# A fused dilated attention and depthwise convolution: the convolution's centre term moved into PSUM, one block's left column moved to VectorE, the exponentials kept in PSUM, and a new order of all stages

## The chip, the cores and the metric

The kernel runs on one core of a Trainium2 chip. The core has five engines with a queue each: TensorE (PE in the profile; its weight loads are PEld), VectorE (DVE), ScalarE (ACT), GpSimd (POOL) and SyncE (SP), which here issues nearly all DMAs. The metric is the device time of one execution in microseconds. Before the change it is 5062.4 us, the median of three runs (5062.21 to 5062.62). A profile is one further execution, recorded by the hardware profiler.

## The reference

Two layers on an image batch `x` of 16 x 56 x 56 x 384 in float32:

```python
    # --- layer 0 (conv_preact) ---
    x = x + _L0_conv_ref(_gn(x), L0_conv_w_qkv, L0_conv_w_proj, L0_conv_b_proj)
    # --- layer 1 (conv_preact) ---
    x = x + _L1_conv_ref(_gn(x), L1_conv_w)
```

`_gn` is a group norm over 32 groups of channels. Layer 0 is a dilated neighbourhood attention: q, k and v are products of the normalised `x` with `w_qkv`; the 384 channels are three groups of 128 (four heads of 32 channels each) with dilations 1, 2 and 3; each pixel attends to the 3 x 3 neighbours at its group's distance,

```python
        attn = jnp.einsum('bgdn,bgdkn->bgnk', qg, ku) * scale
        attn = jax.nn.softmax(attn, axis=-1)
        out = jnp.einsum('bgnk,bgdkn->bgnd', attn, vu)
```

and the result goes through `w_proj` and `b_proj`. Layer 1 is a 3 x 3 depthwise convolution (one kernel per channel) whose weights are the signs of `w`.

## The kernel before

Channels lie on the 128 partitions, in three blocks (j = 0, 1, 2). A chunk is 8 rows of 56 pixels, 448 in all; an image has 7 chunks, the batch 112. A chunk goes through three plans. Plan A (`plan_a`) loads it and turns it to channels first (pt_x, xa) and sends it to DRAM as xd, with running statistics. Plan B (`plan_b`) is the attention; plan C (`plan_c`), some ten chunks later, the convolution.

Plan B, for each of three channel groups: `k_or_v` and `query` are products of three matmuls each on TensorE (L526), into a PSUM tile pkv (pool `ps_mt`) or pq (pool `ps_q`). `score` multiplies pq with three neighbours of k at once on VectorE (t, L591: 1344 elements a partition). `score_rounds` sums each head's 32 channels of t by narrow matmuls into ps (L572; 128x32, four beside each other in the array). `softmax` copies ps (L611), turns it (pt_s, L615), takes the maximum and the difference on VectorE (L620, L621), the exponential on ScalarE (L623), the sum, its reciprocal and the product on VectorE (L627, L628, L630); then the weights are split into three bf16 terms (L633, L636, L640, L641) and turned by a DMA into aT (L644). `weigh`, once for each row of neighbours (i = 0 to 8), spreads the weights over the channels on TensorE into pb_a (L658; pool `ps_bc`, three banks, a single buffer), multiplies by v on VectorE (w, L669) and adds up on GpSimd (L679, L682, L683). `out_project` multiplies with w_proj (po, L696), adds bias and residual (L701), takes statistics (L705) and sends x1 to DRAM.

Plan C: `load` brings each 32 channels of block 0 and 1 three times, shifted by a row (z), `normalise` normalises z on ScalarE (L786). `convolve` makes the left and right columns of the 3 x 3 kernel for blocks 0 and 1 on TensorE: for each of the two columns kx = 0 and 2, and each quarter q, one matmul (pc, L817; 96 rows by 32 columns of the array). The middle column (upper and lower tap: L828, L831) is added on VectorE, on raw x1 with scalars cs that hold kernel times group-norm scale. `column` computes the centre tap with the group norm's offset and the residual on ScalarE into an SBUF tile u (L807), and VectorE adds it last (L834). Block 2 is done without TensorE: nine scaled copies on ScalarE (L881) that GpSimd adds (L891, L896, L899). `turn` turns the result back (pt_o, L908) and writes it out.

[...]The eight banks are: `ps_mt` three (pkv, pt_x, pt_s, po, pc, pt_o and small products of the group norm), `ps_q` one, `ps_s` one (ps, and later the sums psm), `ps_bc` three. A tile that takes a bank waits until the one that had it was read.

The order is written out. `WHEN` gives each stage a place in units of which nine make a chunk (`STEP`); `put` adds these to a chunk's start t0 and splits a stage at its `yield`s. All pieces are sorted by place; between places `FROM` and `UNTIL` every engine's instructions are chained in that order (`pin`), SP's DMAs included. Before the change that is so from chunk 0 on, FROM = 0; pieces with places under 0 or past UNTIL are left to the scheduler. The last image's convolution has its places by itself, after the last statistics, and lies past UNTIL.

Of the kernel before, what the change touches and what calls it, by code (L numbers as in the profile page):

```python
# [8 lines left out]
F32 = mybir.dt.float32  # L9
BF16 = mybir.dt.bfloat16  # L10
I32 = mybir.dt.int32
AF = mybir.ActivationFunctionType
ALU = mybir.AluOpType
# [9 lines left out]
NQ = 4  # L23
ROWS = 8
# [10 lines left out]
    load_in=[[16.753]],  # L35
    turn_in=[[17.144, 17.155, 17.527, 18.442], [18.901, 18.912, 18.923, 27.065], [19.007, 19.044, 19.055,
        19.119]],
    load_x=[[-8.992]],
    normalise=[[-7.557], [-6.631], [-8.034]],
    k=[[-1.772, -1.287, -0.448], [0.602, 0.693, 0.86], [1.389, 1.4, 3.364]],  # L40
    v=[[8.754, 8.765, 10.709], [11.496, 11.507, 13.768], [11.843, 12.429, 17.643]],
    query=[[8.972], [10.387], [12.844]],
    score=[[9.067], [9.078], [9.773], [10.398], [11.394], [12.106], [13.128], [13.334], [13.447]],
    burst=[[10.996], [12.316], [15.131]],
    softmax=[[15.921, 17.148, 17.159, 17.17, 18.062, 18.073, 18.4, 18.411, 18.491, 18.969]],
    weigh=[[20.479, 20.601, 20.612], [20.873, 21.461, 23.801], [21.808, 22.007, 26.039], [23.6, 23.611, 26.895],
        [24.179, 25.026, 27.192], [25.361, 26.931, 28.274], [26.999, 27.767, 29.055], [28.005, 28.036, 29.926],
        [28.762, 28.913, 30.376]],
    load_residual=[[33.194]],
    out_project=[[30.892, 34.249, 34.26, 121.395], [30.995, 34.02, 34.806, 62.468], [36.328, 36.339, 36.805,  # L50
        37.381]],
    load_g=[[15.738]],
    normalise_g=[[20.315]],
    taps=[[23.621, 25.792], [23.781, 25.945], [23.792, 25.956]],
    sums=[[26.625], [26.636], [26.647]],
    load_x1=[[12.088]],
    load_z=[[4.532, 8.639], [18.154, 18.373]],
    normalise_z=[[11.361, 11.372], [19.211, 19.222]],
    column=[[12.191], [16.571]],
    convolve=[[12.055, 12.746], [20.473, 20.484]],  # L60
    turn_out=[[27.033, 27.07, 27.117], [27.209, 27.576, 27.587], [27.767, 27.778, 29.092], [28.344, 28.355,
        36.059]],
    statistics=[[38.5, 42.48, 42.607, 43.359, 44.23, 44.622, 44.633, 44.887, 45.025, 45.117, 45.558, 45.569,
        45.58, 46.991, 47.002]],
# [6 lines left out]
def dilated_attention_then_binary_conv(  # L71
# [48 lines left out]
    ps_mt = ctx.enter_context(tc.tile_pool(name="ps_mt", bufs=3, space=PSUM))  # L120
    ps_q = ctx.enter_context(tc.tile_pool(name="ps_q", bufs=1, space=PSUM))
# [54 lines left out]
    kcol = const.tile([P, JG, 3], F32, name="kcol")  # L176
# [18 lines left out]
    u_p = ctx.enter_context(tc.tile_pool(name="u_p", bufs=1))  # L195
# [79 lines left out]
    def small_weights():  # L275
# [34 lines left out]
        nc.vector.tensor_add(kcol[:, :, 2], up, mid)  # L310
        eye3 = raw["eye"]
# [15 lines left out]
    def rows(ap):  # L327
        return ap.rearrange("p (r w) -> p r w", w=W)
# [114 lines left out]
    def must_hold(what, value):  # L443
        assert holds.get(what) == value, (what, holds.get(what), value)
# [63 lines left out]
    def plan_b(m, t0):  # L508
# [88 lines left out]
        def by_neighbour(ap):  # L597
            return ap.rearrange("p s (o k) -> p s o k", o=NTAP)

        def over_neighbours(ap):  # L600
            return ap.unsqueeze(2).to_broadcast([SUB, NSUB, NTAP, GH])
# [5 lines left out]
        def softmax():  # L607
# [9 lines left out]
            must_hold("ew", m - 1 if m else None)  # L617
# [3 lines left out]
            nc.vector.tensor_tensor(by_neighbour(weights), by_neighbour(pt4), over_neighbours(mx), ALU.subtract)  # L621
            yield
            nc.scalar.activation(weights, weights, AF.Exp, scale=SCALE)  # L623
            yield
            sm = ps_s.tile([P, 512], F32, tag="s", name="psm")[:SUB, : NSUB * GH]
            sm = sm.rearrange("p (s k) -> p s k", s=NSUB)
            nc.vector.reduce_sum(sm, by_neighbour(weights).rearrange("p s o k -> p s k o"), axis=AX.X)  # L627
            nc.vector.reciprocal(sm, sm)  # L628
            yield
            nc.vector.tensor_tensor(by_neighbour(weights), by_neighbour(weights), over_neighbours(sm), ALU.mult)  # L630
# [91 lines left out]
    def column_scalars(b):  # L722

        mr = mr1[b][0]
        cs = st_p.tile([P, JG, 6], F32, tag="cs", name="cs")
        nc.gpsimd.tensor_tensor(
            cs[:, :, 0:3], ktap[:, :JG, 1:NTAP:3], mr[:, :JG, 1:2].to_broadcast([P, JG, 3]), ALU.mult
        )
        nc.gpsimd.tensor_tensor(cs[:, :, 3:6], kcol, mr[:, :JG, 0:1].to_broadcast([P, JG, 3]), ALU.mult)
        nc.gpsimd.tensor_scalar(cs[:, :, 1], cs[:, :, 1], 1.0, None, op0=ALU.add)  # L730
        cs1[b] = cs

    def plan_c(m, t0):
# [17 lines left out]
        def set_of(j, q):  # L751
            return next(z[:, q - q0] for z, q0, q1 in had[f"z{j}"] if q0 <= q < q1)
# [46 lines left out]
        def column(j):  # L799

            x1, cs = had["x1"], cs1[b]
            had["u", j] = u = u_p.tile([P, ROWS, W], F32, tag="u", name="u")
            parts = [(0, 1, 3), (1, ROWS, 4)] if c == 0 else [(0, ROWS, 4)]
            if c == NCH - 1:
                parts = [(0, ROWS - 1, 4), (ROWS - 1, ROWS, 5)]
            for r0, r1, of in parts:
                nc.scalar.activation(  # L807
                    u[:, r0:r1], x1[:, j, r0 + 1 : r1 + 1], AF.Identity, bias=cs[:, j, of : of + 1], scale=cs[:, j, 1:2]
                )

        def convolve(j):
            pc = ps_mt.tile([P, 512], F32, tag="mt", name="pc")
            pcr = rows(pc[:, :PX])

            def tap(kx, q):
                x0, x1 = max(0, 1 - kx), W - max(0, kx - 1)
                return nc.tensor.matmul(  # L817
                    pcr[q * HD : (q + 1) * HD, :, x0:x1], kdiag[:, kx // 2, j * NQ + q, :],
                    rows(set_of(j, q))[:, :, x0 + kx - 1 : x1 + kx - 1], start=(kx == 0), stop=(kx == 2),
                    skip_group_check=True,  # L820
                )

            in_one_go([lambda kx=kx, q=q: tap(kx, q) for kx in (0, 2) for q in (3, 0, 1, 2)])
            yield
            x1 = had["x1"][:, j]
            mid = x1[:, 1 : ROWS + 1]
            cs, above, below = cs1[b], 1 if c == 0 else 0, ROWS - 1 if c == NCH - 1 else ROWS
            nc.vector.scalar_tensor_tensor(  # L828
                pcr[:, above:], x1[:, above:ROWS], cs[:, j, 0:1], pcr[:, above:], op0=ALU.mult, op1=ALU.add
            )  # L830
            nc.vector.scalar_tensor_tensor(  # L831
                pcr[:, :below], x1[:, 2 : below + 2], cs[:, j, 2:3], pcr[:, :below], op0=ALU.mult, op1=ALU.add
            )
            nc.vector.tensor_tensor(mid, pcr, had["u", j], ALU.add)  # L834
            had["conv", j] = True
# [116 lines left out]
    FROM, UNTIL = 0, STEP * N + 14  # L952
# [7 lines left out]
    at(5.14, small_weights)  # L960

# [78 lines left out]
```

## Time and profile before

| what | value |
|---|---|
| median of three runs | 5062.4 us |
| profiled execution: whole time | 5064.99 us |
| profiled execution: span | 5063.3 us |
| mean granted TensorE clock over the span | 0.98 |
| PE weight loads, busy, 420 to 4700 us | 1961.5 of 4280 us |
| PE / DVE / ACT / POOL busy, 420 to 4700 us | 4267.0 / 3912.1 / 2246.6 / 3788.4 us |
| PE / DVE / ACT / POOL busy, 4700 us to the end | 251.9 / 244.1 / 178.3 / 210.1 of 364 us |
| PE waiting for w at pb_a, whole span | 22.6 us, 17 times |
| DVE waiting for pb_a | 164.2 us, 315 times |
| DVE waiting for pq | 98.8 us, 140 times |

The span runs from the first to the last recorded instruction; some 2 us lie around it. Busy times are unions: instructions of one engine may overlap. Each float32 matmul gives two records, so pc has 3360 (105 chunks of 16 matmuls); the last image's are a group of their own (z_last, 224). A wait is idle time of an engine ahead of an instruction, put down to what came last.

### The profile page before, as it was taken

What the parts mean: (1) busy time and instruction counts of PE and PEld (TensorE: products, weight loads), DVE (VectorE), ACT (ScalarE), POOL (GpSimd) and SP (SyncE); (2) the same over time, 40 slices, a digit from 0 to 9 for tenths busy, and PEclk for the clock granted to TensorE, in tenths of its full rate; (3) what the DMA queues carried; (4) which work ended last, traced back from release to release, by engine and by line L of the source; (5) the groups of instructions that cost most, each with busy time, mean ns of one, the idle gap of its engine ahead of it and who ended that gap; (6) DMA issues with size and microseconds to landing.
All of it is one profiled execution on the core that took longest, in us unless ns stands there. A gap on an engine that the chain in (4) does not pass through costs nothing.

```text
span 5063.3 us, 70210 instructions
## 1 busy us (share of the span) xinstructions
PE 4883.1 (96%) x24325; PEld 2249.2 (44%) x24325; DVE 4455.8 (88%) x4559; ACT 2524.2 (50%) x4501; POOL 4224.4 (83%) x2862
## 2 busy tenths in 40 slices
PE   7899999999999999999999999999999999999965
PEld 4444444444444444444444444444444444444422
DVE  4788999999999999999999999999999999888856
ACT  3122555555555555555555555555555555555445
POOL 2577889888898888889888888888889888898970
PEclk9999999999999999999999999999999999999976
DMA  5344666666666666666666666666666666655545
GB/s 155 108 126 118 176 176 172 174 169 176 168 183 172 170 173 170 176 175 182 165 178 176 177 177 176 180 173 172 178 163 182 176 169 174 156 147 141 141 135 153
DMA packets 831098, 836.43 MB, mean 165 GB/s; under 512 B 379796, under 2 KB 800023, under 8 KB 830743
## 3 DMA queue, kind: packets, MB, share of 16 engines
q1 hardware_dynamic: 822758, 819.95, 61.5%
q10 hardware_dynamic: 7984, 12.00, 0.7%
q8 instruction: 192, 3.15, 0.3%
q14 instruction: 164, 1.34, 0.1%
HBM read 477.52 MB, written 231.24 MB: 140 GB/s over the span
## 4 chain that ended last, share of the span: by engine, by line
PE 86%; DVE 4%; DMA 4%; POOL 2%; ACT 2%; SPq 2%; issue 1%; ACTq 0%; DVEq 0%; POOLq 0%
PE pkv L526 27%; PE pq L526 15%; PE po L696 14%; PE ps L572 11%; PE pc L817 6%; PE pb_a L658 5%; PE pt_x L474 3%; PE pt_o L908 3%; DVE t L591 2%; DMA xd<-xa 1%; DVE w L669 1%; PE pt_s L615 1%; ACT z L786 1%; POOL w L679 1%; DMA mrz<-mrd 0%
## 5 line engine op out<-in xcount | busy, mean ns | idle before, releaser
L679 POOL TENSOR_TENSOR w<-w 128x1344 f32<-128x1344 f32 x672 | 2054.6, 3057 | 275.3 <-DVE w L669 268.4
L669 DVE TENSOR_TENSOR w<-pb_a,v 128x1344 f32<-128x1344 f32 x1008 | 1561.4, 1549 | 231.6 <-PE pb_a L658 164.2
L591 DVE TENSOR_TENSOR t<-pq,k 128x1344 f32<-128x1344 f32 x1008 | 1542.2, 1549 | 100.6 <-PE pq L526 98.8
L526 PE MATMUL pkv<-xn,wqkvT 128*128 128x448 f32 x3924 | 1593.0, 547 | 0.0
L526 PEld LDWEIGHTS pkv<-xn,wqkvT 128*128 128x128 f32 x3924 | 718.5, 190 | 644.6 <-issue 623.2
L696 PE MATMUL po<-y,wprojT 128*128 128x448 f32 x2016 | 808.3, 546 | 8.8 <-POOL y L683 8.8
L526 PE MATMUL pq<-xn,wqkvT 128*128 128x448 f32 x1962 | 807.5, 548 | 7.9 <-DVE t L591 7.8
L572 PE MATMUL ps<-t,sel 128*32 128x448 f32 x6048 | 659.0, 545 | 9.4 <-DVE t L591 9.4
L891 POOL TENSOR_TENSOR m<-m 128x1344 f32<-128x1344 f32 x210 | 639.6, 3046 | 27.3 <-ACT m L881 19.1
L786 ACT ACTIVATE z<-z,mrz 96x448 f32<-96x448 f32 x840 | 570.3, 753 | 29.2 <-DMA mrz<-mrd 24.2
L881 ACT ACTIVATE m<-zg,ktap 128x448 f32<-128x448 f32 x945 | 540.7, 658 | 3.6 <-POOL m L891 3.6
L696 PEld LDWEIGHTS po<-y,wprojT 128*128 128x128 f32 x2016 | 378.5, 193 | 351.1 <-issue 320.3
L611 ACT COPY sT<-ps 128x448 f32<-128x448 f32 x112 | 59.8, 534 | 894.8 <-PE ps L572 894.8
L526 PEld LDWEIGHTS pq<-xn,wqkvT 128*128 128x128 f32 x1962 | 354.4, 190 | 312.7 <-issue 300.4
L539 ACT COPY k<-pkv 128x448 f32<-128x448 f32 x336 | 180.9, 538 | 575.4 <-PE pkv L526 574.9
L683 POOL TENSOR_TENSOR y<-y,w 128x448 f32<-128x448 f32 x336 | 382.7, 1139 | 26.3
L682 POOL TENSOR_TENSOR y<-w 128x448 f32<-128x448 f32 x336 | 382.4, 1138 | 26.3
L658 PE MATMUL pb_a<-aT,spread 24*128 24x448 bf16 x3024 | 368.9, 359 | 23.9 <-DVE w L669 22.6
L817 PE MATMUL pc<-z,kdiag 96*32 96x440 f32 x3360 | 360.6, 548 | 28.6 <-ACT z L749 18.8
L658 PEld LDWEIGHTS <-spread 24*128 24x128 bf16 x3024 | 99.8, 91 | 648.7 <-issue 567.1
L914 ACT COPY osb<-pt_o 112x384 f32<-112x384 f32 x420 | 199.1, 474 | 291.9 <-PE pt_o L908 284.3
L636 POOL TENSOR_TENSOR rest<-ew,e 112x512 f32<-112x512 f32 x112 | 129.9, 1159 | 240.1 <-ACT e L633 240.1
(136 smaller groups left out, 4817.6 us busy)
## 6 DMA issues: line engine op xcount, KB each, us to landing
z<-x1d SPq DMA_DIRECT2D x570, 224.0 KB, 4.3
xr<-xd SPq DMA_DIRECT2D x112, 672.0 KB, 4.9
x1d<-xr SPq DMA_DIRECT2D x112, 672.0 KB, 3.5
xn<-xd SPq DMA_DIRECT2D x109, 672.0 KB, 4.8
xin<-in_x_dram SPq DMA_DIRECT2D x105, 672.0 KB, 7.3
xd<-xa SPq DMA_DIRECT2D x315, 224.0 KB, 4.3
out_dram<-osb SPq DMA_DIRECT2D x420, 168.0 KB, 4.1
x<-x1d SPq DMA_DIRECT2D x80, 560.0 KB, 5.2
```

The source lines that it names most:

```text
L526: nc.tensor.matmul(dst[:, :PX], wqkvT[:, cc, o0 : o0 + P], had["xn"][:, cc, :], start=(cc == 0), stop=(cc == NG - 1))
L572: return nc.tensor.matmul(had["ps"][32 * j : 32 * j + 32, :PX], sel[:, s0 : s0 + 32], tk, start=(issued[j] == 1), stop=(issued[j] == len(r ...
L591: nc.vector.tensor_tensor(t.rearrange("p k (r w) -> p k r w", w=W), q3, k3, ALU.mult)
L658: return nc.tensor.matmul(pb[:, kx, :PX].rearrange("p (s n) -> p s n", s=NSUB), spread[rows_of, v % 2, :], had["a"][rows_of, :, v // 8, :] ...
L669: nc.vector.tensor_tensor(w.rearrange("p k (r w) -> p k r w", w=W), pb[:, :, :PX].rearrange("p k (r w) -> p k r w", w=W), three(kv[1][g][m ...
L679: nc.gpsimd.tensor_tensor(w0, w0, w, ALU.add)
L683: nc.gpsimd.tensor_tensor(y, y, w0[:, 2], ALU.add)
L696: nc.tensor.matmul(po[:, :PX], wprojT[:, g, j * P : (j + 1) * P], had[f"y{g}"], start=(g == 0), stop=(g == NG - 1))
L786: nc.scalar.activation(z, z, AF.Identity, bias=mrz[:, j, q, 0:1], scale=mrz[:, j, q, 1:2])
L817: return nc.tensor.matmul(pcr[q * HD : (q + 1) * HD, :, x0:x1], kdiag[:, kx // 2, j * NQ + q, :], rows(set_of(j, q))[:, :, x0 + kx - 1 : x ...
L881: nc.scalar.activation(rows(t[:, kx]), zp[:, ky : ky + ROWS, kx : kx + W], AF.Copy, scale=ktap[:, JG, o : o + 1])
L891: nc.gpsimd.tensor_tensor(had["m"], had["m"], t, ALU.add)
```

## The change

Four edits and a new order. *Convolution:* `column` now writes the centre term straight into the PSUM tile pc, which it takes from pool `ps_q`, and the matmuls of `convolve` add on top (no matmul of it starts a fresh sum). Two matmuls at the start (`open_banks`) write the two banks of `ps_q` once. The last VectorE tap writes x1 itself, the tile u and its pool go. *Left column:* for block 0 (LEFT) the four matmuls of kx = 0 go; VectorE does the three taps, over 55 of 56 columns. Their scalars come from longer tables kcol and cs, and ScalarE's centre term is split into columns 1 to 55 and column 0, with different offsets. *Exponentials:* the difference is written over pt_s in PSUM, ScalarE's exponential goes from there into the bank of ps_s, the sum reads it there and lies in SBUF, and only the product goes to SBUF. *Banks:* `ps_mt` has two, `ps_q` two. *Order:* every place in WHEN is new, with plan C's stages mostly 5 to 10 units later and B's weigh stages 4 to 7 later; FROM is 9 * STEP: the first nine chunks are left to the scheduler.

```diff
 NQ = 4
+LEFT = (0,)
...
-    k=[[-1.772, -1.287, -0.448], [0.602, 0.693, 0.86], [1.389, 1.4, 3.364]],
+    k=[[1.392, 1.555, 1.762], [3.751, 3.762, 5.408], [3.97, 4.507, 7.411]],
...
-    column=[[12.191], [16.571]],
-    convolve=[[12.055, 12.746], [20.473, 20.484]],
+    column=[[21.708], [24.774]],
+    convolve=[[22.545, 23.258], [24.904, 25.733]],
...
-    ps_mt = ctx.enter_context(tc.tile_pool(name="ps_mt", bufs=3, space=PSUM))
-    ps_q = ctx.enter_context(tc.tile_pool(name="ps_q", bufs=1, space=PSUM))
+    ps_mt = ctx.enter_context(tc.tile_pool(name="ps_mt", bufs=2, space=PSUM))
+    ps_q = ctx.enter_context(tc.tile_pool(name="ps_q", bufs=2, space=PSUM))
...
-            must_hold("ew", m - 1 if m else None)
...
-            nc.vector.tensor_tensor(by_neighbour(weights), by_neighbour(pt4), over_neighbours(mx), ALU.subtract)
-            yield
-            nc.scalar.activation(weights, weights, AF.Exp, scale=SCALE)
-            yield
-            sm = ps_s.tile([P, 512], F32, tag="s", name="psm")[:SUB, : NSUB * GH]
-            sm = sm.rearrange("p (s k) -> p s k", s=NSUB)
-            nc.vector.reduce_sum(sm, by_neighbour(weights).rearrange("p s o k -> p s k o"), axis=AX.X)
+            nc.vector.tensor_tensor(by_neighbour(pt4), by_neighbour(pt4), over_neighbours(mx), ALU.subtract)
+            yield
+            pe = ps_s.tile([P, 512], F32, tag="s", name="psm")[:SUB]
+            ex = pe[:, : NSUB * NR].rearrange("p (s v) -> p s v", s=NSUB)
+            sm = s_p.tile([SUB, NSUB, GH], F32, tag="mx", name="sm")
+            nc.scalar.activation(ex, pt4, AF.Exp, scale=SCALE)
+            yield
+            nc.vector.reduce_sum(sm, by_neighbour(ex).rearrange("p s o k -> p s k o"), axis=AX.X)
             nc.vector.reciprocal(sm, sm)
             yield
-            nc.vector.tensor_tensor(by_neighbour(weights), by_neighbour(weights), over_neighbours(sm), ALU.mult)
+            must_hold("ew", m - 1 if m else None)
+            nc.vector.tensor_tensor(by_neighbour(weights), by_neighbour(ex), over_neighbours(sm), ALU.mult)
...
-            had["u", j] = u = u_p.tile([P, ROWS, W], F32, tag="u", name="u")
+            had["pc", j] = pc = ps_q.tile([P, 512], F32, tag="q", name="pc")
+            pcr = rows(pc[:, :PX])
...
-                nc.scalar.activation(
-                    u[:, r0:r1], x1[:, j, r0 + 1 : r1 + 1], AF.Identity, bias=cs[:, j, of : of + 1], scale=cs[:, j, 1:2]
-                )
+                for x0, x_end, more in ((1, W, 6), (0, 1, 0)) if j in LEFT else ((0, W, 0),):
+                    nc.scalar.activation(
+                        pcr[:, r0:r1, x0:x_end], x1[:, j, r0 + 1 : r1 + 1, x0:x_end], AF.Identity,
+                        bias=cs[:, j, of + more : of + more + 1], scale=cs[:, j, 1:2],
+                    )
...
-            in_one_go([lambda kx=kx, q=q: tap(kx, q) for kx in (0, 2) for q in (3, 0, 1, 2)])
+            in_one_go([
+                lambda kx=kx, q=q: tap(kx, q) for kx in ((2,) if j in LEFT else (0, 2)) for q in (3, 0, 1, 2)
+            ])
...
+            taps = [(above, ROWS, 0, 0, 0)]
+            if j in LEFT:
+                taps += [(above, ROWS, 0, 6, 1), (0, ROWS, 1, 7, 1), (0, below, 2, 8, 1)]
+            for r0, r1, ky, at_, left in taps:
+                acc = pcr[:, r0:r1, left:]
+                nc.vector.scalar_tensor_tensor(
+                    acc, x1[:, r0 + ky : r1 + ky, : W - left], cs[:, j, at_ : at_ + 1], acc, op0=ALU.mult, op1=ALU.add
+                )
             nc.vector.scalar_tensor_tensor(
-                pcr[:, above:], x1[:, above:ROWS], cs[:, j, 0:1], pcr[:, above:], op0=ALU.mult, op1=ALU.add
-            )
-            nc.vector.scalar_tensor_tensor(
-                pcr[:, :below], x1[:, 2 : below + 2], cs[:, j, 2:3], pcr[:, :below], op0=ALU.mult, op1=ALU.add
-            )
-            nc.vector.tensor_tensor(mid, pcr, had["u", j], ALU.add)
+                mid[:, :below], x1[:, 2 : below + 2], cs[:, j, 2:3], pcr[:, :below], op0=ALU.mult, op1=ALU.add
+            )
+            if below < ROWS:
+                nc.vector.tensor_copy(mid[:, below:], pcr[:, below:])
...
-    FROM, UNTIL = 0, STEP * N + 14
+    FROM, UNTIL = 9 * STEP, STEP * N + 14
...
+    def open_banks():
+        for _ in range(2):
+            pq = ps_q.tile([P, 512], F32, tag="q", name="pq")
+            nc.tensor.matmul(pq[:, :PX], ident, wqkvT[:, 0, :PX], start=True, stop=True)
```

## The prediction

> **What bounds the kernel now.** I read the page first (busy shares, then the chain that ended last), then the chain in order of time, then one chunk in the timelines of TensorE and VectorE, then the tail.
>
> ```profile
> PE 4883.1 (96%) x24325; PEld 2249.2 (44%) x24325; DVE 4455.8 (88%) x4559; ACT 2524.2 (50%) x4501; POOL 4224.4 (83%) x2862
> ```
> ```profile
> 2476.82 4.51 PE po L696 x12
> ...
> 2519.13 4.51 PE po L696 x12
> ```
> ```profile
> 2504.47:2546.78 42.31, 42.31 (x216) 19.46 (x216) 38.92 (x38) 22.67 (x40) 37.39 (x21) 1.00 0.67 177
> ```
>
> The same link of the chain returns after 42.31 us: that is one chunk. In just that stretch (columns: length, then busy time of PE, weight loads, VectorE, ScalarE, GpSimd) PE is busy all 42.31 us, VectorE 38.92, GpSimd 37.39, ScalarE 22.67. So TensorE sets the pace, and VectorE has 3.4 us to spare. An image is seven chunks and one set of statistics: between two po links of the chain, 1707.25 and 2007.69, lie 300.4 us, 4.3 more than seven chunks. Outside this: the filling (first pc at 503.2) and the tail (last pkv begins at 4816.7 of 5063.3, 247 us, GpSimd full up to 4900, then a chain of loads and short steps).
>
> Busy time of matmuls overlaps; the price of a group is the distance from its start to the next start:
>
> ```profile
> 2504.76 1.71 PE L572 MATMUL ps<-t,sel 128*32 128x448 f32 x16
> 2506.29 1.66 PE L817 MATMUL pc<-z,kdiag 96*32 96x440 f32 x16
> 2507.89 0.36 PE L658 MATMUL pb_a<-aT,spread 24*128 24x448 bf16 x3
> 2508.18 4.78 PE L526 MATMUL pkv<-xn,wqkvT 128*128 128x448 f32 x12
> 2512.89 0.36 PE L658 MATMUL pb_a<-aT,spread 24*128 24x448 bf16 x3
> 2513.19 1.68 PE L817 MATMUL pc<-z,kdiag 96*32 96x440 f32 x16
> 2514.69 1.69 PE L572 MATMUL ps<-t,sel 128*32 128x448 f32 x16
> 2516.31 0.36 PE L658 MATMUL pb_a<-aT,spread 24*128 24x448 bf16 x3
> ```
>
> A pc of eight matmuls (16 records, two for each) takes 1.50 us before ps and 1.60 before pb. VectorE's half of the convolution:
>
> ```profile
> 2508.02 0.69 DVE L828 SCALAR_TENSOR_TENSOR pc<-x,cs,pc 128x448 f32<-128x448 f32 x1
> 2508.75 0.69 DVE L831 SCALAR_TENSOR_TENSOR pc<-x,cs,pc 128x448 f32<-128x448 f32 x1
> 2509.47 0.62 DVE L834 TENSOR_TENSOR x<-pc,u 128x448 f32<-128x448 f32 x1
> 2510.01 1.55 DVE L669 TENSOR_TENSOR w<-pb_a,v 128x1344 f32<-128x1344 f32 x1
> ```
>
> A step that needs the one before it starts 0.73 us after it; the last lets go after 0.54; one block costs 1.99 us, two 3.98. In the same way t and w cost 1.465 each (of 1.549), a bn_stats 0.53.
>
> **The change, part by part.** *Left column off TensorE.* Four of sixteen pc matmuls a chunk go. 1.55/2 = 0.78 us of PE per chunk, all on the path. What is left of block 0 (four matmuls) now stands alone between pb and pq, without ps beside it. [...]The rows show the size: 1.60 against 1.50. [...]by the rows one more run of narrow matmuls costs 0.1, and the net is 0.7.
>
> *The new order* (every stage of WHEN moves) brings TensorE more: three-matmul groups of full width cost 2.26 us beside each other and 2.35 next to a pb. In the old order eight such sides touch a pb, in the new one, read off the built program, five: 0.3 us. Adding all groups of the new cycle at these paces (twelve full groups 27.1, five sides 0.5, nine pb 2.7, ps and pc 7.9, transposes 3.1) gives 41.3 us; the same sum over the old order gives 42.3, as measured.
>
> *VectorE* takes three taps (8 rows by 55 elements). Nearest rows: 392 elements 0.630, 448 elements 0.687; unknown is whether rows of 55 cost more. Ends 0.60 (no dependence) and 0.80; I take the dependent pace 0.73. L834 goes, since the last tap writes x1 itself. Block 0: 4 x 0.73 + 0.60 = 3.52, block 1: 0.73 + 0.60 = 1.33, together 4.85 against 3.98, +0.87.
>
> *Exponentials in PSUM.* The sum changes its source:
>
> ```profile
> L627 DVE TENSOR_REDUCE psm<-ew 112x48 f32<-112x432 f32 x112 | 102.1, 911 | 0.7 <-ACT ew L623 0.7
> ...
> L620 DVE TENSOR_REDUCE mx<-pt_s 112x48 f32<-112x432 f32 x112 | 67.9, 606 | 33.1 <-PE pt_s L615 33.1
> ```
>
> The new sum has the form of the second row (PSUM in, SBUF out): 0.911 becomes 0.606, -0.30. [...]By the row VectorE gains 0.3 a chunk, [...]I take the row, whose shape is the same. Subtraction, exponential and product are taken at their old durations (0.607, 0.564, 0.594); 0.1 either way. VectorE in all: 38.92 + 0.87 - 0.30 = 39.5 of 41.3: 95%.
>
> *Does that fit?* pb_a has one buffer: the pb of neighbour group 1 waits for w of the old chunk's last group. In the new program VectorE does, from the third po's L701 to that w: 0.60 + nine t and w 13.19 + two bn 1.06 + convolution 4.85 + 0.09 (end of the last) = 19.8, with handovers of 0.20 (pq group's end 2518.96, t at 2519.16) and 0.05 it is 20.05. TensorE has between the same points: pkv twice 4.52, pt_x 0.47, pb 0.29, pc 0.83, pq and pkv 4.52, pt_x 0.46, pb 0.29, ps 1.53, pc 1.60, pb 0.30, pkv 2.35, pq 2.26, pt_o 0.35 = 19.8. So PE will wait some 0.25 us there: **41.55 us a chunk, 0.76 saved**.
>
> *Banks.* mt goes from three to two, q from one to two and holds pc too. Each mt tile must be evacuated while one other group runs. Three places have under 0.2 us: pkv behind the second pt_o, the first po behind the copy of v, the second po behind the exponential, which now keeps the bank of pt_s (0.2 + 0.65 + 0.61 + 0.57 + handovers = 2.1 in 2.26). I take 0, at worst 0.25 each. The new wait of pc for ScalarE's column has over 1 us: ScalarE is half idle, and the split column (0.76 and, from the 56-element row, 0.43) hides there.
>
> *GpSimd and DMA.* GpSimd gets two 0.2 us instructions per image, hidden in its 4.9 us of slack (3.9 at 41.3). No DMA is added. SP's queue is reordered; the tight one is the transpose to aT (4.1 us to land): after GpSimd's last part of e3 some 6.5 us remain to its first pb. The new places of halo and load DMAs leave over 2 us each: nothing.
>
> *Statistics.* 4.3 us now, of them 2.3 matmuls. VectorE's part (0.74 twice and small ones) falls on a VectorE with 2 us of slack, not 3.4: I add 0.7, 14 times: +10.
>
> *Filling.* The first chunks, in a fixed order before, are left to the scheduler; it splits some groups (some 25 breaks at 0.1). The two matmuls that open banks run while PE waits for loads. Taken +5, from -10 to +20.
>
> *Tail.* The work left behind the last ps is nearly the same (GpSimd two m sums more, 6 us). But the column now comes first:
>
> ```profile
> 4974.77 5.23 DMA x<-x1d
> 4980.72 0.68 DVE pc L828
> ```
>
> Before, pc was ready when x1 landed; now x1 must land, then ScalarE (1.1), then pc, then up to five taps. Some 4 us more at each of three x1 loads on the chain, less 4 for pc groups there that lose a quarter: +8; with GpSimd half hidden, +10; range 0 to +30.
>
> **Sum.** 105 chunks have the convolution with a running pipeline, less four behind the last pkv: 101 x 0.76 = 77. 77 - 10 - 5 - 10 = 52 saved. The profiled execution has a span of 5063.3 in 5065.0 us; the median is 5062.4, so the same cut is made there: **5010 us**.
>
> **Rivals.** *VectorE closes a loop, and it is slower.* If the two engines wait for each other as before (VectorE idle 3.4 a chunk, only partly because there was nothing to do), a chunk takes 39.5 + 3.4 = 42.9: 101 x 0.6 = 60 lost, 25 more as above, 5147; it decides once VectorE's idle time stays above 2.8 a chunk, and a lesser form (3.0) gives 5107. For it: VectorE would be the fullest engine, with a chain through the single pb buffer that is already 0.25 over. Against it: in the new order most of its waits find their data there.
>
> *Two mt banks eat the gain.* Three tight places at 0.15 each: 0.45 a chunk, 45 back: 5055; at 0.05 it is hardly seen. For it: 17 mt tiles a chunk; against: ScalarE waits for PE nearly everywhere now (k L539 alone 574.9 us).
>
> *More is gained.* Without the 0.25 wait and with filling and tail even: 101 x 1.0 = 101, 4961.
>
> **How the numbers follow.** Forecast and its neighbourhood (4985 to 5040) 0.58; more gained 0.12; banks 0.17; VectorE's loop 0.13. A measurement of this kernel tells from no change what differs by over 0.2% (10 us: 5052 to 5073). Faster: 0.58 + 0.12, 0.08 of the banks, 0.02 of the loop = 0.80; same: 0.08 of the banks, 0.01 of the loop = 0.09; slower 0.11. The range 4955 to 5062 takes in the gain case and most of the banks' and leaves the loop out.
>
> **What would show it.** Right: pc records of z 2520 instead of 3360; the po link of the chain returning after 41.4 to 41.7; VectorE near 95% in one chunk; the sum at 0.61; waits of pb for w grown from 22.6 to some 30 to 45 us, at one group. Wrong: a lone pc that takes over 0.9; taps over 0.75; po waiting for the exponential in each chunk; a tail over 265 us from the last pkv; a first pc later than the extra two thirds of a chunk explains (503 to some 530).

## The result: a small gain where a large one was forecast, and the profile after

In 20 runs each the kernel takes 5051.7 us after the change (5047.03 to 5059.69) and 5060.26 us before it (5056.47 to 5071.2): a ratio of 0.9983, with a 95% interval of 0.9976 to 0.9989. The forecast was 5010, 52 us less than before; 8.6 us came. The profiled execution's span fell by more than the median, from 5063.3 to 5048.7 us; the account below is of these two traces, 14.6 us apart. The mean granted TensorE clock is 0.98 in both, and 1.00 in the chunks that are compared next, so it has no part in the difference of a chunk.

Busy shares of the page after, to be laid beside those of before:

```profile
PE 4833.2 (96%) x23433; PEld 2213.7 (44%) x23433; DVE 4513.4 (89%) x4710; ACT 2573.4 (51%) x4645; POOL 4226.0 (84%) x2894
```

TensorE has 892 records fewer and is still 96% busy. One chunk of the windows view, from one first po to the next (length; then busy time of PE, weight loads, VectorE, ScalarE, GpSimd; then clock, DMA share, GB/s):

```profile
2503.40:2545.35 41.95, 41.95 (x207) 19.20 (x206) 39.93 (x42) 23.03 (x41) 37.34 (x21) 1.00 0.67 181
```

A chunk takes 41.95 us where it took 42.31, and TensorE is busy in all of it: no wait at all. (VectorE's 39.93 hold 0.7 of the group norm's sums that fall into this chunk; an ordinary one has 39.3.) So 0.35 us a chunk was gained, not 0.76, and no wait took the rest. It lies in TensorE's own sum, the distances from the start of each group of matmuls to the next. A full group is one of three full-width matmuls (po, pkv, pq). Its side is an edge at which narrower matmuls (pb, ps, pc) stand next to it; a short transpose can have such sides too. TensorE's timeline after, around what moved (start, busy time, records):

```profile
2510.71 4.67 PE L530 MATMUL pkv<-xn,wqkvT 128*128 128x448 f32 x12
2515.22 0.55 PE L478 MATMUL pt_x<-ident,xin 112*128 112x112 f32 x4
2515.70 0.36 PE L663 MATMUL pb_a<-aT,spread 24*128 24x448 bf16 x3
2516.00 0.95 PE L825 MATMUL pc<-z,kdiag 96*32 96x440 f32 x8
2516.87 2.52 PE L530 MATMUL pq<-xn,wqkvT 128*128 128x448 f32 x6
...
2530.72 0.36 PE L663 MATMUL pb_a<-aT,spread 24*128 24x448 bf16 x3
2531.01 1.71 PE L576 MATMUL ps<-t,sel 128*32 128x448 f32 x16
2532.66 0.43 PE L924 MATMUL pt_o<-ident,x 128*112 128x128 f32 x2
2532.92 0.27 PE L924 MATMUL pt_o<-ident,xg 128*112 128x128 f32 x1
2533.13 0.36 PE L663 MATMUL pb_a<-aT,spread 24*128 24x448 bf16 x3
2533.42 0.60 PE L478 MATMUL pt_x<-ident,xin 112*128 112x112 f32 x4
2533.86 2.43 PE L530 MATMUL pkv<-xn,wqkvT 128*128 128x448 f32 x6
```

And a pt_o before, ahead of a full group and behind another transpose:

```profile
2541.84 0.38 PE L908 MATMUL pt_o<-ident,x 128*112 128x128 f32 x2
...
2542.17 2.42 PE L526 MATMUL pq<-xn,wqkvT 128*128 128x448 f32 x6
```

The lone pc of block 0 takes 0.87 us from its start to the next start. A pt_o (three transposes) takes 0.33 where only full groups and transposes touch it (2541.84 to 2542.17), in both kernels; between a full group and a pb it takes 0.42, between ps and pb 0.47 (2532.66 to 2533.13). Before, three of the four pt_o of a chunk took 0.33 and one 0.37; after, one takes 0.33 and three 0.42 to 0.47. A pt_x (four transposes) has a pb beside it in both kernels: 0.48 ahead of it (2515.22 to 2515.70), 0.44 behind it.

VectorE's new instructions, from the view of groups by shape (count, busy time, mean ns, idle time before):

```profile
L843 DVE SCALAR_TENSOR_TENSOR pc<-x,cs,pc 128x440 f32<-128x440 f32 x304 | 206.8, 680 | 10.0
L631 DVE TENSOR_REDUCE sm<-psm 112x48 f32<-112x432 f32 x112 | 66.2, 591 | 0.7 <-ACT psm L629 0.7
```

A tap over 55 columns takes 0.680 us, the sum 0.591 where it took 0.911. Last, of the waits of all engines between 600 and 4450 us, two of PE and one of ACT (total, times, longest):

```profile
ACT z L792 <- DMA mrz<-mrd: 21.1, 13, 2.2
...
PE pb_a L663 <- DVE w L674: 17.7, 13, 1.5
...
PE pt_x L478 <- ACT k L543: 14.5, 12, 1.8
```

They come 12 or 13 times, once for each image: nearly all the waiting TensorE does in this stretch (33.2 us) is at the statistics. In the same stretch before, neither of PE's two was there, only 7.0 us in all, 6.6 of them of pc for ScalarE's edge of z. ScalarE's wait for the scalars is not new. Before, it was

```profile
ACT z L786 <- DMA mrz<-mrd: 18.8, 13, 2.6
```

Copies of k and v stood behind it then too, and TensorE waited for none of them. In after it does. One such place in ScalarE's timeline:

```profile
1702.81 2.72 ACT L792 ACTIVATE z<-z,mrz 96x448 f32<-96x448 f32 x4 [1.51 <-DMA mrz<-mrd]
1705.43 1.88 ACT L815 ACTIVATE pc<-x,cs 128x55 f32<-128x55 f32 x4
1707.24 0.52 ACT L543 COPY k<-pkv 128x448 f32<-128x448 f32 x1
```

The copy of k frees the bank that pt_x takes, and pt_x starts at 1707.82, after a wait of 1.07 us.

**Where the 14.6 us come from.** By the starts of the first po: chunk 10 is reached at 584.5 us, not 593.5, so the filling gained 9.0. From chunk 10 to 101 are 91 chunks and 13 statistics: 3886.1 us against 3892.1. The chunks gained 91 x 0.35 = 32; so the statistics gave back 26, 2.0 an image, as much as TensorE's waits grew there (33.2 against 7.0). From chunk 101 to the end both need 578 us.

### The profile page after: what moved, and what is told of

It reads as the page before. It is cut to its first block, busy times and chain, and to the rows that moved or that the text cites. A ratio compares the mean times of both kernels' runs of the same rounds, so it can differ in the third digit from the quotient of the medians.

```text
span 5048.7 us, 69318 instructions
## 1 busy us (share of the span) xinstructions
PE 4833.2 (96%) x23433; PEld 2213.7 (44%) x23433; DVE 4513.4 (89%) x4710; ACT 2573.4 (51%) x4645; POOL 4226.0 (84%) x2894
## 4 chain that ended last, share of the span: by engine, by line
PE 81%; POOL 7%; DVE 3%; DMA 3%; issue 3%; ACT 2%; SPq 0%; ACTq 0%; POOLq 0%; DVEq 0%
PE pkv L530 26%; PE pq L530 14%; PE po L701 13%; PE ps L576 11%; PE pb_a L663 5%; PE pc L825 5%; POOL w L684 3%; PE pt_o L924 3%; PE pt_x L478 3%; DVE w L674 1%; DMA mrd<-mr 1%; POOL m L907 1%; DVE t L595 1%; PE pt_s L619 1%; DMA mrz<-mrd 1%
## 5 line engine op out<-in xcount | busy, mean ns | idle before, releaser
L701 PE MATMUL po<-y,wprojT 128*128 128x448 f32 x2016 | 822.7, 553 | 12.1 <-ACT osb L930 7.2
L543 ACT COPY v<-pkv 128x448 f32<-128x448 f32 x336 | 180.1, 536 | 977.6 <-PE pt_o L924 487.5
L792 ACT ACTIVATE z<-z,mrz 96x448 f32<-96x448 f32 x840 | 569.8, 750 | 26.2 <-DMA mrz<-mrd 21.1
L701 PEld LDWEIGHTS po<-y,wprojT 128*128 128x128 f32 x2016 | 359.5, 191 | 346.7 <-issue 256.8
L663 PE MATMUL pb_a<-aT,spread 24*128 24x448 bf16 x3024 | 369.7, 360 | 55.6 <-DVE w L674 46.2
L843 DVE SCALAR_TENSOR_TENSOR pc<-x,cs,pc 128x440 f32<-128x440 f32 (+3 forms) x560 | 376.1, 673 | 31.7 <-issue 8.6
L576 PEld LDWEIGHTS ps<-t,sel 128*32 128x32 f32 x6048 | 169.5, 109 | 295.4 <-issue 285.5
```

Source lines behind the costliest of these rows:

```text
L576: return nc.tensor.matmul(had["ps"][32 * j : 32 * j + 32, :PX], sel[:, s0 : s0 + 32], tk, start=(issued[j] == 1), stop=(issued[j] == len(r ...
L663: return nc.tensor.matmul(pb[:, kx, :PX].rearrange("p (s n) -> p s n", s=NSUB), spread[rows_of, v % 2, :], had["a"][rows_of, :, v // 8, :] ...
L701: nc.tensor.matmul(po[:, :PX], wprojT[:, g, j * P : (j + 1) * P], had[f"y{g}"], start=(g == 0), stop=(g == NG - 1))
L792: nc.scalar.activation(z, z, AF.Identity, bias=mrz[:, j, q, 0:1], scale=mrz[:, j, q, 1:2])
```

## The experiments

Each ratio is to before on the same chip; after itself has 0.9983. "Steady" is the distance of first po links in the chunks away from the statistics.

### Is the order or the left column mis-sized?

Two kernels: after with the left column back on TensorE (left_back), and before with it left out (left_out_old; nothing takes its place, and block 0's right column runs over all 56 columns, in lines that the diff leaves out).

```diff
-LEFT = (0,)
+LEFT = ()
```
```diff
-            in_one_go([lambda kx=kx, q=q: tap(kx, q) for kx in (0, 2) for q in (3, 0, 1, 2)])
+            in_one_go([lambda kx=kx, q=q: tap(kx, q) for kx in ((2,) if j == 0 else (0, 2)) for q in (3, 0, 1, 2)])
```

> After, with the left column of block 0 back on TensorE (four more matmuls a chunk; the three taps and the split column go), all else and the order as after. Theory A (the new order itself makes TensorE dearer: seven full-width runs a chunk between narrow work where there were six, and transposes standing alone): the chunk goes from 41.96 to about 42.7 us, above the 42.31 of before; 5125 to 5135 us in all. Theory B (the prediction's: the new order saves TensorE 0.3 us, and it is the left column's cut that is lost somewhere): about 42.1 us a chunk, 5060 to 5070.

> Before, in its old order and with its old banks, with the four matmuls of block 0's left column left out (the right column's matmuls run on 56 unshifted columns; nothing takes the place of the left column). Theory A: the cut is worth nearly its whole price there, because block 0's pc stands beside ps: 42.31 less 0.72 to 0.78 is 41.55 us a chunk, about 4985 us. Theory B (something else limits as soon as TensorE has less): 42.0 us a chunk or more, above 5025.

Measured: left_back 5091.09 us, ratio 1.0066 (1.0054 to 1.0079), steady 42.69; left_out_old 4982.12 us, 0.9851 (0.9838 to 0.9865), steady 41.58. The windows view of left_back:

```profile
2441.92:2484.61 42.69, 42.69 (x215) 19.50 (x214) 37.41 (x36) 22.31 (x39) 37.77 (x24) 1.00 0.62 170
```

TensorE is full, with VectorE at 37.4: nothing else limits. The column is worth 42.69 - 41.95 = 0.74 us a chunk in the new order and 42.31 - 41.58 = 0.73 in the old. The new order costs TensorE 42.69 - 42.31 = 0.38 with the same matmuls. Adding start-to-start distances by kind over one chunk shows where:

| us a chunk | before | left_back | after | forecast for after |
|---|---|---|---|---|
| twelve full groups (po, pkv, pq) | 27.86 | 27.74 | 27.74 | 27.6 (27.1 and sides 0.5) |
| transposes (pt_x, pt_o, pt_s) | 3.16 | 3.54 | 3.53 | 3.1 |
| ps and pc | 8.64 | 8.77 | 8.03 | 7.9 |
| pb | 2.65 | 2.65 | 2.65 | 2.7 |
| sum | 42.31 | 42.70 | 41.95 | 41.3 |

The order does take narrow neighbours away from full groups (-0.12), but puts transposes in their place (+0.38), and pc and ps have more sides too (+0.13). Most of the +0.38 is the four pt_o (1.65 us a chunk after, 1.36 before). left_back also keeps the new banks and the exponentials in PSUM, but TensorE shows no wait in that chunk (busy 42.69 of 42.69 us) that they could have caused. So theory A is shown: the left column's price came in full, and the new order is the dearer one. left_back's total stayed under its forecast mainly because an image takes only 3.6 us more than seven chunks there, 5.3 in after, 3.3 before. So of the 2.0 us an image that the statistics gave back, 1.7 came with the left column's work on VectorE and ScalarE, and 0.3 with the order and the banks: TensorE's pt_x waits 3.9 us for k in left_back, 14.5 in after.

### Fewer sides: does TensorE gain by them?

In pc_by_ps block 0's pc goes behind the longest ps burst, in after_pt_o_joined the pt_o between ps and pb goes into the run of full groups behind it, in pt_o_joined both. With pc move the loads of its z, and one v product goes ahead of the pq that it followed (two lines that the first diff leaves out).

```diff
...
-    normalise_z=[[21.293, 22.164], [23.971, 24.249]],
-    column=[[21.708], [24.774]],
-    convolve=[[22.545, 23.258], [24.904, 25.733]],
+    normalise_z=[[25.7, 25.71], [23.971, 24.249]],
+    column=[[28.65], [24.774]],
+    convolve=[[28.69, 32.258], [24.904, 25.733]],
```
```diff
-    turn_out=[[36.858, 36.869, 36.88], [37.053, 37.1, 37.526],
+    turn_out=[[36.858, 36.869, 36.88], [37.41, 37.556, 37.78],
```

> After, with block 0's convolution moved behind the longest burst of ps (so that it no longer stands alone between pb and pq), its column copy and normalisation of z moved later on ScalarE, the taps on VectorE where they were, and one v projection ahead of the pq it followed. Theory A: one full-width run less, 0.12 us a chunk, and ScalarE no longer waits for the group norm's scalars ahead of a copy of k, 1.0 us in each of 13 images: 41.84 us a chunk, about 5025 us. Theory B (VectorE or the two mt banks set the pace in this order): no chunk under 41.95, 5045 us or more.

> pc_by_ps with the second pt_o moved from its place alone between ps and pb into the full-width run behind it (after the first pkv of the next chunk, ahead of pq). Theory A: against pc_by_ps one full-width run less, 0.2 to 0.3 us a chunk less on TensorE, of which pb may give back up to 0.15 since its w is not ready sooner: 42.4 to 42.55 us a chunk against 42.65. Theory B (a lone transpose costs the same anywhere): 42.65.

> After, with only the second pt_o (three short transposes that stand alone between ps and pb) moved into the full-width run behind it, after the first pkv and ahead of pq. Theory A (each full-width run between narrow work costs its two sides, 0.13 us or more, whatever stands in it): the group leaves 0.47 us and costs 0.33 beside others, so TensorE's sum falls by 0.14 to 0.27; pb waits up to 0.14 for w: 41.75 to 41.9 us a chunk, 5 to 19 us in all. Theory B (the transposes cost the same anywhere, or VectorE, 39.9 us busy with 2.0 of waits, holds the pace): 41.95 us a chunk, no change.

Measured: pc_by_ps 5122.45 us, 1.0126 (1.0111 to 1.0142), steady 42.65; pt_o_joined 5149.56 in its one run, 42.67; after_pt_o_joined 5067.5, 1.001 (1.0002 to 1.0019), steady 41.97. Neither gained. In pc_by_ps the pc did what it should: behind the burst, ps and pc take 3.13 us where the burst took 2.39 and the lone pc 0.87, 0.13 less. But TensorE now waited in each chunk: behind a pb, pkv started 0.40 late, for the bank that ScalarE's copy of xa frees, and pq 0.33 late, for VectorE's t. In after_pt_o_joined the price of the transposes fell from 3.53 to 3.39 us a chunk, as their sides say, but ps and the wait behind it grew by 0.16; why is seen further on (after_pt_o_bn).

Three kernels mended what their traces named. pc_by_ps_2 puts the copy of k ahead of that of xa and a bn_stats behind a t; pc_by_ps_3 puts the chunk's first t ahead of a w as well (score 11.334 to 11.1); all_joined adds the joined pt_o and a later copy of the group norm's result.

> pc_by_ps with two places mended that its trace shows waiting in every chunk: the copy of k goes ahead of the copy of xa on ScalarE (TensorE waited 0.39 us there for a bank of mt), and one statistics step of plan A goes behind the last t of the query group on VectorE (TensorE waited 0.33 us there for the bank of pq). Theory A: both waits go, 42.65 falls to 41.85 us a chunk, some 5030 us in all; one full-width run less is worth 0.1. Theory B (VectorE is full, so the waits only turn up elsewhere): 42.2 us or more.

> pc_by_ps_2 with one more place: on VectorE the first t of a chunk goes ahead of the w that waits for the pb behind ps and pc. Theory C (what held pc_by_ps and pc_by_ps_2 at 42.65 although TensorE had stalls at different places is VectorE: pc behind the long burst keeps the single pb buffer back, and VectorE stands 1.9 us there, not 0.5): the wait falls to 0.5, and the chunk to 41.8 to 41.9 us, 5030 us. If TensorE's own sum were 42.65 there, no change: 5122.

> pc_by_ps_3 with the second pt_o joined as in after_pt_o_joined, and VectorE's copy of the group norm's result one t later (VectorE stood 1.6 us an image for it). Theory A: five full-width runs fewer sides, 41.6 to 41.75 us a chunk, statistics 2 us an image less: about 5000 to 5015 us. If VectorE is the bound by then (39.9 busy and its fixed waits): 41.9, 5025 us.

Measured: 5125.43 (1.0123), 5124.02 (1.0123) and 5145.31 us (1.016); steady 42.65, 42.64 and 42.66. Three misses: the named waits went and others came, the chunk stayed to within 0.02, and theory C fell too. VectorE's timeline of pc_by_ps_2, around the stretch in which it has no gap (idle time before an instruction stands in brackets):

```profile
2466.55 0.68 DVE L706 SCALAR_TENSOR_TENSOR xr<-po,bias,xr 128x448 f32<-128x448 f32 x1 [0.39 <-PE po L701]
2467.14 1.55 DVE L595 TENSOR_TENSOR t<-pq,k 128x1344 f32<-128x1344 f32 x1
...
2495.19 1.56 DVE L674 TENSOR_TENSOR w<-pb_a,v 128x1344 f32<-128x1344 f32 x1 [0.46 <-POOL w L684]
2498.62 1.56 DVE L674 TENSOR_TENSOR w<-pb_a,v 128x1344 f32<-128x1344 f32 x1 [1.88 <-PE pb_a L663]
```

From 2466.55 to 2494.7, VectorE never waits. It starts on the third po of TensorE, and within it TensorE's pq (0.18 us late at 2482.99) and pb (0.26 late at 2486.30) wait for VectorE's t and w. A loop runs through both engines: TensorE's work from the last such pb to the next third po, then VectorE's. In after both sides need the same time. From the end of the third po (2510.71) to the pb at 2530.72 TensorE takes 20.0 us. The w that this pb needs is

```profile
2529.06 1.55 DVE L674 TENSOR_TENSOR w<-pb_a,v 128x1344 f32<-128x1344 f32 x1
```

It lets go 1.47 us after its start, at 2530.53, and where a pb waits for a w it starts 0.14 after that (2464.64 to 2464.78 in after_pt_o_joined): 2530.67, only 0.05 before the pb did start. So when pc left TensorE's side of the stretch, 0.05 could be gained there, and pc's 0.74 came on top elsewhere: 41.95 + 0.74 - 0.05 = 42.64. The five kernels with pc moved have 42.64 to 42.67. This fits, but it is worked out; the next runs test it.

### Taking VectorE out of the loop

Two of VectorE's six statistics steps a chunk (bn_stats) go to places behind the stretch, alone and with each cut. The kernels with pc moved have the copy of k ahead of that of xa as well.

```diff
-    turn_in=[[22.335, 22.469, 24.701, 28.875], [23.943, 25.409, 27.06, 27.63], [28.352, 28.363, 28.599,
+    turn_in=[[22.335, 22.469, 27.985, 28.875], [23.943, 25.409, 27.06, 27.63], [28.352, 28.363, 28.599,
...
-    out_project=[[38.334, 38.803, 38.814, 140.965], [39.193, 39.204, 39.638, 45.624], [39.633, 39.644, 40.418,
-        44.585]],
+    out_project=[[38.334, 38.803, 38.814, 140.965], [39.193, 39.204, 39.638, 45.624], [39.633, 39.644, 46.3,
+        46.45]],
```

> After, with two of VectorE's six bn_stats (0.53 us each) moved out of the stretch from the third po to the last w of the chunk (20 us in which VectorE has no gap) to places behind it where it has waits. Theory D (in after both engines are exactly full there: TensorE without a gap all through the chunk, VectorE through this stretch): alone it gives nothing, 41.95 us a chunk, because TensorE's own sum is 41.95. Theory E (VectorE's chain alone sets 41.95): 41.4 us or less, 5000 us.

> pc_by_ps (42.65 us a chunk, with the copy of k ahead of that of xa) with the two bn_stats moved. Theory D: VectorE's stretch was what took 0.8 us back when pc left TensorE's side of it; with 1.06 less on it, TensorE's sum rules again, 41.95 less 0.87 for pc alone plus 0.74 for pc behind ps: 41.8 us a chunk. Otherwise 42.65 stays, or falls by less than half of that.

> after_pt_o_joined (41.97 us a chunk) with the two bn_stats moved. Theory D: the wait of pb for w (0.25 us in every chunk) goes, and the joined pt_o is worth its whole cut on TensorE, 0.57 less 0.32: 41.7 us a chunk. Rival (a lone transpose group costs TensorE the same anywhere): 41.95.

> pc_by_ps_bn with the second pt_o joined and x1's load earlier. Theory D: 41.8 less 0.25 is 41.55 us a chunk if VectorE's stretch, shorter by 1.06 but with TensorE's side shorter by 1.4, does not bind again; as it should by up to 0.3: 41.6 to 41.9.

after_bn_moved: 5040.28 us, 0.9968 (0.9958 to 0.9979), steady 41.95. As theory D has it, VectorE alone does not set the chunk. What it gained is at the statistics (pb's wait for w 17.7 to 8.0 us, the span 5048.7 to 5038.6); the interval just touches that of after, so this gain rests on the traces.

pc_by_ps_bn: 5124.64 us, 1.013 (1.0116 to 1.0144), no less than pc_by_ps_2. Most of the three chunks ahead of the statistics take 42.35 to 42.4 us, but the two before those mostly 42.7 to 43.0. At best a quarter of a microsecond came off, not 0.8: theory D's number did not come. The waits of PE name one reason:

```profile
PE pt_o L924 <- POOL xg L915: 26.3, 64, 0.7
```

TensorE comes to the first pt_o before GpSimd has its last sum: the group takes 0.92 us there, not 0.42. Without these 0.5 the chunk would be 41.89, if nothing else bound. The next kernel moves the first two pt_o one place on each, and x1's load ahead:

> pc_by_ps_bn with the first two pt_o one place later each (the first between ps and pb, the second in the full-width run behind it), so that they no longer come before GpSimd's last sum, and x1's load earlier. Theory D: the 0.5 us wait of pt_o for GpSimd goes, and 42.39 falls to TensorE's own sum, 41.85 to 41.9 us a chunk. If GpSimd or VectorE then binds elsewhere: 42.1 or more.

It took 5111.85 us, 1.0099 (1.0085 to 1.0113), steady 42.21: the wait for GpSimd went, but pb waited for w in 87 chunks (43.0 us in all). So less work in VectorE's stretch and a later pt_o together took 0.44 off (42.65 to 42.21), and TensorE's own sum of 41.9 was not reached. The later pt_o was not tried without the bn_stats. That VectorE holds these kernels up is seen in pb's waits; that the loop is the whole of the 0.7 us is not shown.

after_pt_o_bn: 5043.38 us, 0.997 (0.9958 to 0.9982), steady still 41.97, although VectorE now had slack. all_bn, with both cuts: 5157.65 us, 1.0198 (1.0184 to 1.0212), 42.4 to 43.2 a chunk; TensorE waits for GpSimd (25.9 us), VectorE (23.1) and ScalarE (21.8). For after_pt_o_bn the answer is in the timelines of TensorE and VectorE:

```profile
2492.64 0.36 PE L663 MATMUL pb_a<-aT,spread 24*128 24x448 bf16 x3
...
2494.73 0.37 PE L663 MATMUL pb_a<-aT,spread 24*128 24x448 bf16 x3
```

```profile
2491.69 0.62 DVE L493 BATCH_NORM_STATS2 stats<-xa 128x6 f32<-128x448 f32 x1
2493.12 1.56 DVE L674 TENSOR_TENSOR w<-pb_a,v 128x1344 f32<-128x1344 f32 x1 [0.82 <-PE pb_a L663]
2494.60 3.01 DVE L595 TENSOR_TENSOR t<-pq,k 128x1344 f32<-128x1344 f32 x2
```

VectorE waits 0.82 us for the first pb and starts w at once; the next pb starts 2.09 us after the first. pb has one buffer, which the next pb takes when w has read it, and 2.07 to 2.09 us is the shortest distance of two pb in these traces, before's too (2.07 at 255.38, 2.08 at 294.95). Between the two stood ps (1.53) and pt_o (0.47); with pt_o gone, pb waits 0.25, and pt_o costs its 0.33 in the other place. The lone transposes, which looked like waste, filled a wait. Theory D's reason for this kernel fell.

### The old order with the new arithmetic

The places are before's, but for these three lines:

```diff
+    load_x1=[[10.5]],
+    column=[[12.2], [19.9]],
+    convolve=[[12.318, 12.746], [20.473, 20.484]],
```

> After's arithmetic, banks and start in before's order of stages: only the column copies are moved ahead of their matmuls, block 0's matmuls behind the ps burst that they stood ahead of, and the load of x1 1.6 places earlier. Theory A (the old order is the cheaper one for TensorE, six full-width runs a chunk and not seven, and VectorE's added work fits beside it): the chunk takes 41.6 us as with the left column left out, the whole 4985 to 5000 us. Theory B (VectorE at 39.5 of 41.6, or two mt banks in an order laid out with three, make TensorE wait): 42.0 us a chunk or more, 5040 us or more, with waits of TensorE for ScalarE's copies or for w in every chunk.

Measured 5531.09 us, 1.0924 (1.0909 to 1.0938), steady 46.9 or 45.3, from chunk to chunk. Theory A's number was far off, B's right in sign. VectorE has 39.5 us of work in 47, and TensorE's long ps burst waits for t:

```profile
2627.74 4.15 PE L576 MATMUL ps<-t,sel 128*32 128x448 f32 x22 [2.04 <-DVE t L595]
```

The first taps stand right behind their pc, as before placed them, and there are more of them now in VectorE's queue, ahead of the t that ps waits for (165.8 us in all, 81 times). Copies of ScalarE hold TensorE in nearly each chunk as well (pt_x for k 24.1 us, po for osb 19.5, 81 times each). These two, and the number of banks, were not separated, so whether the old order can carry the new arithmetic with other small moves stays open.

### What the statistics cost more

```diff
-        56.694, 57.245, 57.256]],
+        56.12, 56.6, 57.256]],
...
-    load_x1=[[21.201]],
+    load_x1=[[20.5]],
```

The first edit alone is scalars_early, both are scalars_early_2; best_mix is both with the two bn_stats moved and the copy of k ahead of that of xa.

> After, with the last steps of the statistics earlier: the scalars' two DMAs issue 2.7 us sooner, everything else as after. If ScalarE's wait for those scalars (21.1 us in 13 images), and the pt_x that waits for a bank behind it, is what the statistics cost more: that wait goes, pt_x no longer waits, 12 to 20 us are saved, 5032 to 5040 us, steady chunk unchanged at 41.96. If VectorE's own statistics work sets the delay, or the DMA now blocks SP: 5047 us or more.

> scalars_early with x1's load ahead of the scalars' DMAs in SP's queue. In scalars_early ScalarE waited 1.05 us for x1 in 12 images, because that load stood behind the DMA that waits for the first one. If the late copy of k behind ScalarE's wait is what pt_x waits for (9.0 us are left of 14.5): pt_x no longer waits, another 5 to 9 us, about 5034 us on a chip where after has 5048. If pt_x's wait comes from VectorE's statistics work: no change from scalars_early.

> After, with the two bn_stats moved (after_bn_moved), the scalars' DMAs and x1's load earlier (scalars_early_2) and the copy of k ahead of that of xa. If the two delays at the statistics are separate (VectorE's w 0.7 us an image, ScalarE's scalars and the late copy of k 0.8 us): 41.95 us a chunk, an image 297.5 us against 299.1, about 20 us under after: 5030 us where before has 5060, ratio 0.994 or less. If they are one delay seen from two engines: no better than either, 0.996.

Measured: scalars_early 5042.67 us, 0.9972 (0.996 to 0.9983); scalars_early_2 5036.95, 0.995 (0.9938 to 0.9963); best_mix 5034.5, 0.995 (0.9936 to 0.9963), all with 41.95 in the steady chunk. scalars_early fell short of the 12 to 20 us that were expected: its wait for the scalars fell to 1.1 us in all, and another came for it:

```profile
ACT pc L815 <- DMA x<-x1d: 12.6, 12, 1.9
PE pt_x L478 <- ACT k L543: 9.0, 10, 1.6
```

x1's load stood behind the scalars' second DMA on SP, which waits for the first. With the load ahead of it, ScalarE no longer waits for x1, but for the scalars again (9.7 us); pt_x waits 6.6 us, and in best_mix 3.9, with pb's wait for w at 8.4. By the traces the mean image falls from 298.9 (after) to 298.4, 298.2 and 297.4 us, the span from 5048.7 to 5039.7, 5039.5 and 5030.3. So in the profiles the two delays look separate: their gains add, though part of best_mix's may be the copy of k, which was not moved alone. The medians of best_mix and scalars_early_2 cannot be told apart. Both are faster than before and than after.

## Why the prediction was wrong, step by step

- **Left column off TensorE**, net 0.7: right. 0.74 in this order, 0.73 in the old one. The lone pc costs 0.10 more than one beside ps (0.87 against 0.77 in left_out_old), as the rows said.
- **The new order brings 0.3**: this is the step that failed. "Adding all groups of the new cycle at these paces" gave 41.3; TensorE takes 41.95 without a wait. The prediction carried the transposes over at 3.1 us, and they take 3.53; the full groups were 0.14 and ps and pc 0.13 too low. It counted five sides of full groups at a pb, rightly, but not a sixth at the lone pc, and it did not price the sides of the transposes, which now stand where full groups stood. The order costs 0.38 with the same matmuls. So the forecast chunk, 42.31 - 0.7 - 0.3 + 0.25 for a wait, was 41.55, and the measured one is 42.31 - 0.74 + 0.38 = 41.95.
- **VectorE** 39.5 us, 95%: right (39.3, 94%). Taps follow each other at 0.72 (0.73 said), the sum takes 0.591 (0.606 said): the row was right.
- **pb waits 0.25 for w**: not in an ordinary chunk of after, since TensorE's stretch takes 20.0 us, not 19.8, beside VectorE's 20.0. The error in TensorE's sum thus hid a quarter of a microsecond of itself. The sign given for this wait, 30 to 45 us in all, nearly came (46.2 us over the span), but by luck: 17.7 of it is at the statistics and 26.2 behind 4450 us, near the end. VectorE and TensorE full side by side in one stretch was the right picture; it shows as soon as something is taken from TensorE.
- **Banks**, 0: right for the ordinary chunk. At the statistics a late copy of k, which frees one of the two banks, holds up pt_x (14.5 us in all); whether a third bank would have hidden that was not tried, and left_back, with the same two, has 3.9.
- **Statistics**, 0.7 an image: too small; 2.0. (The 4.3 us of before was read from one image; the mean is 3.3.) VectorE's share was thought of; ScalarE's wait for the scalars, about as long before, was not; through the copy of k behind it, it now holds up TensorE.
- **Filling**, 5 us lost: it gained 9.0, and why is not shown. **Tail**, 10 us lost from the last pkv: 13.6 (247 to 260.6 us), but mostly because the last pkv stands 12 us earlier in the new order. From the first po of chunk 109 to the end it was 240.4 us and is 242.0.
- **The sum**: 77 - 10 - 5 - 10 = 52. In the traces 32 - 26 + 9 - 0.4 = 14.6, with 91 of the 101 chunks in the first term. The first two terms, 45 and 16 us too high, carry the miss. Of the rivals none came: VectorE's loop did not slow the chunk, and TensorE waited for a bank in none of the ordinary chunks.

## What to carry to other kernels

When an order changes, price every group of the new sequence by what stands on either side of it, the short ones too: here three short transposes cost 0.33 us inside a full-width run and 0.42 to 0.47 at its side. Where two engines are full at once, find the stretch of each and the loop between them before taking work from one: here a cut was worth its full price (the left column, 0.74 us a chunk), nothing (the joined pt_o, 41.97 against 41.95) or less than nothing (the moved pc, 42.65), and the loop is what fits the last. Waits that come once per image count like those in each chunk (2.0 us an image lost, 1.5 of it won back by best_mix); look for what stands behind the late DMA in the same queues.

## What the hardware showed unasked

A ps burst of 11 narrow matmuls ahead of a pc takes 2.25 us (pc_by_ps, 2578.79 to 2581.04), one of 8 takes 1.53 (before, 2504.76 to 2506.29), and a pc of 8 ahead of a ps 1.50. The kernel lays four beside each other, and they overlap: the 16 records of 8 matmuls, 0.54 us each, end within 1.71. A third round of only three thus costs 0.72 to 0.75, as much as a round of four. With one buffer of pb, the next pb came no sooner than 2.07 to 2.09 us after the last (0.48 from its start to that of w, 1.47 for w, 0.14 to the next pb, in after_pt_o_bn). The exponentials' sum over 432 elements is a third shorter from PSUM to SBUF (0.591 us, after) than from SBUF to PSUM (0.911, before); which end makes the difference was not tried.
